# Layer 0's first convolution weights as seven products of quarters per chunk, with sums and bias on GpSimd and finer, interleaved stages

## The chip, the cores and the metric

The kernel runs on one core of a Trainium2 chip. The metric is the time of one execution in device microseconds (us). The five engines of the core are named as the profile names them: PE (matrix products; PEld is its weight load), DVE (VectorE), ACT (ScalarE), POOL (GpSimd) and SP (issues most DMAs). Each engine works through its own queue in order, and waits on semaphores for the others.

## The reference, cut to what matters

Four graph layers follow each other, each with a layer norm in front and a residual. Only layer 0 is touched, and of it only the first part: `x` has 128 graphs of 64 nodes with 256 features.

```python
h = jnp.maximum(_layernorm(x, axis=-1), 0.0)
# layer 0, _L0_gnn_ref(h, adj, Wg0, bg0, Wg1, bg1, ...)
h = relu(einsum('ts,bsh->bth', adj, x @ Wg0 + bg0))   # x is the normed h here
h = relu(einsum('ts,bsh->bth', adj, h @ Wg1 + bg1))
for p in range(1, 5):      # four small LSTMs over windows of p nodes
    ...
```

All numbers are float32. The 256x256 product with `Wg0` is what the change rewrites.

## The kernel before, in words

The 8192 rows (graph and node) are cut into 16 chunks of 512 (`NCH`, `CHUNK`). The first stage of the kernel, from its start to about 193 us, is the two graph convolutions of layer 0; then come layer 0's LSTMs, and layers 1, 2 and 3.

A chunk `n` goes through `graph_convolutions(n)`, a generator with five stages:

1. **norm**: `bn_stats`/`bn_aggr` (L87, L88) on DVE, a root on ACT (L95), two small DVE operations (L96, L97), and four scaled ReLUs on ACT (L109), which give `h`. Then the load of chunk `n + 3` is issued on SP.
2. **aggregate**: eight products of `h` with the block-diagonal adjacency `bdA` (128x128 each) into two PSUM banks, and two DVE copies of 128x512 to `aggT` (L145).
3. **first weights**: per half `c` of the output features two products of 128x512 with `wg0`; the bias comes in with DVE's `scalar_tensor_tensor` (L516, `rsum * bg0 + p`), then a ReLU on ACT (L524). The result is `h1T`.
4. **second weights**: eight products of 128x256 with `wg1`, two DVE additions of `bg1` (L539); the result `z` lies in `aggT`'s buffer.
5. **second aggregation**: eight products of `z` with `bdA`, two ReLUs on ACT (L555), and from chunk 8 on a DMA to `hmem`.

All these products stand in the profile as L50, the helper `mm`. The loop over `n` advances the newest chunk by one stage and then each older one by one stage, so that five chunks are under way. Between these steps it advances `tables`, generators that build lookup tables for layers 1 and 2, mostly with small and 128x512 operations on DVE, and some products on PE. At `n == 2` it issues the LSTM weights `Weights(...)`: three 1 MB loads, and for each four sums of 128x512 on POOL (L440). PSUM has eight banks, taken in turn by `bank()`. The order that is written down is not the order in which instructions stand: a scheduler reorders within each engine's queue, and after that each queue runs strictly in its order.

The LSTMs already use seven products of quarters (`gate`, L651), with sums of weights by the same four operations on POOL.

Of the kernel before, what the change touches and what calls it, by code (L numbers as in the profile page):

```python
# [9 lines left out]
F32 = mybir.dt.float32  # L10
# [3 lines left out]
ALU = mybir.AluOpType  # L14
AX = mybir.AxisListType

P = 128
T = 64
# [12 lines left out]
def gnn_stack_kernel(ctx: ExitStack, tc: tile.TileContext, a: dict, out: bass.AP):  # L31
    nc = tc.nc
    NTOK = out.shape[0]
    NCH = NTOK // CHUNK
# [8 lines left out]
    def bank():  # L43
        return psums["now"].tile([P, 512], F32, tag="bank", name="bank", bufs=psums["banks"])
# [4 lines left out]
    def mm(o, lhsT, rhs, start=True, stop=True):  # L49
        nc.tensor.matmul(o, lhsT, rhs, start=start, stop=stop)  # L50
# [75 lines left out]
    def quarter_sums(v, s):  # L126


        a11, a12, a21, a22 = v[:, 0, :, 0, :], v[:, 1, :, 0, :], v[:, 0, :, 1, :], v[:, 1, :, 1, :]
        for o, x, y, op in (  # L130
            (s[:, 0], a21, a22, ALU.add),
            (s[:, 1], s[:, 0], a11, ALU.subtract),
            (s[:, 2], a12, s[:, 1], ALU.subtract),
            (a21, a11, a21, ALU.subtract),
        ):
            nc.gpsimd.tensor_tensor(o, x, y, op)
        return {1: a11, 2: a12, 3: s[:, 2], 4: a22, 5: s[:, 0], 6: s[:, 1], 7: a21}

    def aggregate(h, bd, dst):

        for c in range(2):
            p = bank()
            for i in range(4):
                mm(p[:, i * P : (i + 1) * P], h[:, i, c * P : (c + 1) * P], bd)
            nc.vector.tensor_copy(dst[:, c, :], p)  # L145
# [269 lines left out]
    with ExitStack() as l0:  # L415
# [37 lines left out]
        with ExitStack() as conv:  # L453
            psums["now"] = conv.enter_context(
                tc.tile_pool(name="psum0", bufs=8, space=bass.MemoryType.PSUM, reuse_waits="tile")
            )

            def cpool(name, bufs):
                return conv.enter_context(tc.tile_pool(name=name, bufs=bufs, reuse_waits="tile"))

            xin = cpool("xin", 4)
            g0 = cpool("g0", 5)
            wc = cpool("wc", 1)
            hop = cpool("hop", 3)

            def load_x(n):
                xt = xin.tile([P, 4, D], F32, tag="xin", name="xin")
                nc.sync.dma_start(out=xt, in_=token_tiles(a["x"], n))
                return xt


            coming = {0: xin.tile([P, 4, D], F32, tag="xin", name="xin")}
            first_x = token_tiles(a["x"], 0)
            for i in range(4):
                nc.sync.dma_start(out=coming[0][:, i, :], in_=first_x[:, i, :])
            for src_, dst_ in (("adjT", adjT2), ("adj", adj2)):
                for h in range(2):
                    nc.scalar.dma_start(out=dst_[h * T : (h + 1) * T, :], in_=a[src_])
            coming[1] = load_x(1)
            wg0 = wc.tile([P, 2, D], F32, tag="wg0", name="wg0")  # L480
            nc.sync.dma_start(out=wg0, in_=a["Wg0"])
            bg0 = wc.tile([P, 2], F32, tag="bg0", name="bg0")
            nc.scalar.dma_start(out=bg0, in_=a["bg0"])
            wg1 = wc.tile([P, 2, D], F32, tag="wg1", name="wg1")
            nc.sync.dma_start(out=wg1, in_=a["Wg1"])
            bg1 = wc.tile([P, D], F32, tag="bg1", name="bg1")
            nc.scalar.dma_start(out=bg1, in_=a["bg1"].partition_broadcast(P))
            for n in (2, 3):
                coming[n] = load_x(n)
            nc.sync.dma_start(out=bias, in_=a["bih"])  # L490
            nc.sync.dma_start(out=bias2, in_=a["bhh"])
            for h in range(2):
                r = slice(h * T, (h + 1) * T)
                nc.gpsimd.tensor_copy(bdA[r, r], adjT2[r, :])

            rsum = wc.tile([P, T], F32, tag="rsum", name="rsum")
            p = bank()
            mm(p[:, :T], ones[:T, :], adjT2[:T, :])
            nc.vector.tensor_copy(rsum, p[:, :T])
            rsum_b = rsum.unsqueeze(1).to_broadcast([P, 8, T])  # L500

            def graph_convolutions(n):

                h = Norm(coming.pop(n), True).all()
                if 4 <= n + 3 < NCH:
                    coming[n + 3] = load_x(n + 3)
                yield
                aggT = g0.tile([P, 2, CHUNK], F32, tag="aggT", name="aggT")
                h1T = g0.tile([P, 2, CHUNK], F32, tag="h1T", name="h1T")
                aggregate(h, bdA, aggT)  # L510
                yield
                for c in range(2):
                    p = bank()
                    for k in range(2):
                        mm(p, wg0[:, k, c * P : (c + 1) * P], aggT[:, k, :], k == 0, k == 1)
                    nc.vector.scalar_tensor_tensor(  # L516
                        h1T[:, c, :].rearrange("p (b t) -> p b t", t=T),
                        rsum_b,
                        bg0[:, c : c + 1],
                        p.rearrange("p (b t) -> p b t", t=T),  # L520
                        ALU.mult,
                        ALU.add,
                    )
                    nc.scalar.activation(h1T[:, c, :], h1T[:, c, :], AF.Relu)  # L524
                yield
                z = aggT.rearrange("p c t -> p (c t)").rearrange("p (i d) -> p i d", i=4)
                for ip in range(2):
                    p = bank()
                    for i2 in range(2):
                        i = 2 * ip + i2  # L530
                        for k in range(2):
                            mm(
                                p[:, i2 * D : (i2 + 1) * D],
                                h1T[:, k, i * P : (i + 1) * P],
                                wg1[:, k, :],
                                k == 0,
                                k == 1,
                            )
                    nc.vector.tensor_tensor(  # L539
                        z[:, 2 * ip : 2 * ip + 2, :],  # L540
                        p.rearrange("p (i d) -> p i d", i=2),
                        bg1.unsqueeze(1).to_broadcast([P, 2, D]),
                        ALU.add,
                    )
                yield
                if n < NCH // 2:
                    col = n % 2 * CHUNK
                    dst = hTs0[n // 4][:, n % 4 // 2, :, col : col + CHUNK]
                else:
                    dst = hop.tile([P, 2, CHUNK], F32, tag="hop", name="hop")  # L550
                for c in range(2):
                    p = bank()
                    for i in range(4):
                        mm(p[:, i * P : (i + 1) * P], z[:, i, c * P : (c + 1) * P], bdA)
                    nc.scalar.activation(dst[:, c, :], p, AF.Relu)  # L555
                if n >= NCH // 2:
                    nc.sync.dma_start(out=hmem[n], in_=dst)

            tables = chain(edge_tables(), late_tables())
            under_way = []  # L560
            for n in range(NCH + 4):
                if n < NCH:
                    under_way.append(graph_convolutions(n))

                for one in under_way[-1:] + under_way[:-1] if n < NCH else list(under_way):
                    if next(one, 0) == 0:
                        under_way.remove(one)
                    if n >= 3:
                        next(tables, None)
                if n == 2:  # L570
                    weights["ih", 0], weights["ih", 1] = Weights("ih", 1), Weights("ih", 2)
                    weights["hh", 1] = Weights("hh", 2)
                    nc.vector.tensor_tensor(bias, bias, bias2, ALU.add)
            for _ in tables:
                pass
# [244 lines left out]
        for slot in range(len(tasks) + 2):  # L820
# [9 lines left out]
            if new:  # L830
                step = steps[new[0]]
                one = step.gate(new[1])
# [12 lines left out]
            if new:  # L845
                next(one)
                flight.append((new, one))
                at, k = new[0], new[2]
# [6 lines left out]
                if step.w == MAX_SKIP and step.t == 2 and k < 2 and step.g < NGR - 1:  # L855
                    for u in range(2):
                        n = 4 * step.g + 2 * u + k
                        later.append((slot, "x", n))
            while later and later[0][0] <= slot:
                _, kind, n = later.pop(0)  # L860
                residual[n] = fetch_x(n)
            next(norm_steps, None)
            while later_weights and later_weights[0][0] <= slot:
                _, ph = later_weights.pop(0)
# [23 lines left out]
    with ExitStack() as l1:  # L888
# [30 lines left out]
        for g, c in last_outs:  # L919
            for u in range(2):  # L920
                n = 4 * g + 2 * u + c
# [447 lines left out]
    with ExitStack() as l2:  # L1369
# [48 lines left out]
        with ExitStack() as dense2:  # L1418
# [60 lines left out]
            side, rights = {}, {}  # L1479
            NP = NCH // 2  # L1480
            with ExitStack() as first_dense:
# [40 lines left out]
                for slot, (pr, m2) in enumerate(tasks):  # L1522
                    n = slot + 3
                    one = first_layer(pr, m2)
# [92 lines left out]
            for pr in range(2, NP):  # L1617
# [4 lines left out]
                one = second_layer(pr, False)  # L1622
# [370 lines left out]
```

## Time and profile before

| what | value |
|---|---|
| time, median of 3 runs | 2060.63 us (2059.19 to 2062.6) |
| the profiled execution's own time | 2061.03 us |
| its span in the profile | 2059.3 us |
| granted TensorE clock, mean | 0.996 |
| busy share of the span: PE, DVE, ACT, POOL | 97%, 66%, 58%, 15% |
| last product of the convolutions starts | 190.82 us |
| first product of the LSTMs starts | 192.77 us |

The page gives busy times and shares, then the span in 40 slices, then groups of instructions. A group's row has the line, engine, operation and tiles, the number of instructions, the busy time and mean duration of one, and the idle time of the engine ahead of them with what ended it. A float32 product stands in the profile as two passes, so "x8" for products with `wg0` means four of them. The timeline gives start and duration; a row merges instructions of one kind. A product's duration holds its drain, so that the distance from one start to the next is the price of one.

### The profile page before, as it was taken

To read this page: it belongs to the slowest core of one execution; us is meant where nothing else is said; L and a number is where in the kernel's file an instruction comes from. 1 tells how busy PE (TensorE), PEld (TensorE's weight loads), DVE (VectorE), ACT (ScalarE), POOL (GpSimd) and SP (SyncE) were. 2 spreads that over 40 slices of the span, in tenths; PEclk is the share of its full clock that TensorE was granted. 3 is DMA by queue.
4 is the path that set the end of the run, shared out by engine and by line. 5 is a ranking of instruction groups with operands and counts; after the bars stand their busy time and mean duration, and the time that the engine had idled before them with its cause. 6 is when DMAs were issued, how large, how long until landed. Compare 5 with 4: busy or idle time off the path is not lost. (4 is left out here: it accounts for less than half of the span.)

```text
span 2059.3 us, 25491 instructions
## 1 busy us (share of the span) xinstructions
PE 2006.1 (97%) x9444; PEld 1346.1 (65%) x9444; DVE 1359.5 (66%) x2507; ACT 1184.4 (58%) x2230; POOL 308.2 (15%) x416
## 2 busy tenths in 40 slices
PE   8999999999999999999999999999999999999998
PEld 6777478866688845887667887333334775444786
DVE  8755666564565477566556555677777877886776
ACT  4344766555565457566446564666675556591544
POOL 3000010020110020002001000323223420000563
PEclk9999999999999999999999999999999999999999
DMA  9331000100100170001001003412223841022012
GB/s 316 98 98 51 0 21 1 42 0 1 41 1 1 40 246 21 1 0 42 0 1 41 1 16 120 138 61 97 72 98 122 298 154 52 0 82 82 32 62 72
DMA packets 63196, 135.06 MB, mean 66 GB/s; under 512 B 6240, under 2 KB 40928, under 8 KB 60768
## 3 DMA queue, kind: packets, MB, share of 16 engines
q1 hardware_dynamic: 56832, 109.11, 15.6%
q0 software_dynamic: 5632, 24.12, 3.1%
q8 instruction: 74, 1.21, 0.2%
q14 instruction: 50, 0.41, 0.1%
q10 hardware_dynamic: 608, 0.20, 0.0%
HBM read 87.28 MB, written 46.14 MB: 65 GB/s over the span
## 5 line engine op out<-in xcount | busy, mean ns | idle before, releaser
L651 PE MATMUL pa<-xop,sih 128*128 128x256 f32 (+2 forms) x1056 | 344.4, 418 | 11.7 <-DVE gate L705 8.2
L679 ACT ACTIVATE gate<-gate,bias 128x256 f32<-128x256 f32 (+2 forms) x368 | 247.4, 679 | 173.6 <-DVE gate L695 91.0
L651 PEld LDWEIGHTS pa<-xop,sih 128*128 128x128 f32 x1056 | 198.4, 190 | 87.9 <-issue 22.8
L651 PE MATMUL pc<-xop,wih 128*128 128x256 f32 (+2 forms) x736 | 251.2, 423 | 0.0
L695 DVE TENSOR_TENSOR gate<-pb,gate 128x256 f32<-128x256 f32 (+2 forms) x184 | 87.5, 475 | 225.7 <-PE pb L651 154.1
L651 PE MATMUL pa<-lstm_h,shh 128*128 128x256 f32 (+1 forms) x672 | 212.7, 398 | 0.0
L993 DVE SCALAR_TENSOR_TENSOR lr<-lr 128x1024 f32<-128x1024 f32 x128 | 151.1, 1222 | 55.3 <-ACT lr L992 55.3
L651 PEld LDWEIGHTS pc<-xop,wih 128*128 128x128 f32 x736 | 139.8, 190 | 51.2 <-issue 23.0
L710 DVE TENSOR_TENSOR gate<-pc,gate 128x256 f32<-128x256 f32 (+2 forms) x184 | 87.6, 476 | 121.2 <-PE pc L651 120.9
L992 ACT COPY lr<-pair 128x1024 f32<-128x1024 f32 x128 | 123.1, 1014 | 47.6 <-PE pair L986 47.6
L651 PEld LDWEIGHTS pa<-lstm_h,shh 128*128 128x128 f32 x672 | 127.7, 190 | 30.2
L651 PE MATMUL pc<-lstm_h,whh 128*128 128x256 f32 (+1 forms) x448 | 141.8, 398 | 0.0
L694 ACT COPY gate<-pa 128x256 f32<-128x256 f32 (+2 forms) x184 | 76.1, 413 | 96.7 <-PE pa L651 96.1
L986 PE MATMUL pair<-sd_hot,xq 64*128 64x512 f32 x512 | 127.5, 616 | 0.3 <-ACT lr L992 0.3
L705 DVE TENSOR_TENSOR gate<-pa,gate 128x256 f32<-128x256 f32 (+2 forms) x184 | 87.5, 475 | 44.0 <-PE pa L651 43.4
L970 PE MATMUL bank<-wlv,hT 128*128 128x512 f32 x240 | 110.7, 604 | 0.0
L699 ACT COPY gate<-pa 128x256 f32<-128x256 f32 (+2 forms) x184 | 75.4, 410 | 59.1 <-PE pa L651 57.9
L679 ACT ACTIVATE gate<-pa,bias 128x256 f32<-128x256 f32 (+2 forms) x184 | 94.0, 511 | 23.6 <-PE pa L651 22.0
L440 POOL TENSOR_TENSOR sih<-wih 128x512 f32<-128x512 f32 x8 | 10.7, 1335 | 630.6 <-DMA wih<-in_WihT 484.4
L651 PE MATMUL pa<-xop,wih 128*128 128x256 f32 (+1 forms) x320 | 101.4, 398 | 2.7 <-ACT xop L632 2.7
L651 PE MATMUL pb<-xop,wih 128*128 128x256 f32 (+1 forms) x320 | 100.3, 398 | 0.4 <-DVE gate L695 0.4
L651 PEld LDWEIGHTS pc<-lstm_h,whh 128*128 128x128 f32 x448 | 85.1, 190 | 20.1
(346 smaller groups left out, 3809.2 us busy)
## 6 DMA issues: line engine op xcount, KB each, us to landing
field<-sd_hot SPq DMA_DIRECT2D x4, 2304.0 KB, 17.2
wih<-in_WihT SPq DMA_DIRECT2D x8, 1024.0 KB, 5.1
xres<-in_x SPq DMA_DIRECT2D x16, 512.0 KB, 4.6
xa<-xres POOLq DMA_DIRECT2D x16, 512.0 KB, 5.2
dense<-field POOLq DMA_DIRECT2D x4, 2048.0 KB, 8.5
xin<-xb SPq DMA_DIRECT2D x16, 512.0 KB, 3.4
h<-xb SPq DMA_DIRECT2D x16, 512.0 KB, 3.2
xin<-in_x SPq DMA_DIRECT2D x15, 512.0 KB, 3.9
```

Source lines behind the costliest of these rows:

```text
L440: nc.gpsimd.tensor_tensor(o, x, y, op)
L651: ins = nc.tensor.matmul(p[:, : self.N], weights[kind, self.phase](k, q), x[k], start=first_ and kind == "ih", stop=kind == "hh" or not se ...
L679: nc.scalar.activation(out, in_, AF.Tanh if q == 2 else AF.Sigmoid, bias=bias[:, self.w - 1, 2 * q + j : 2 * q + j + 1],)
L694: nc.scalar.copy(blk[0, 0], pa[:, :N])
L695: nc.vector.tensor_tensor(blk[0, 0], pb[:, :N], blk[0, 0], ALU.add)
L699: nc.scalar.copy(blk[1, 0], pa[:, :N])
L705: nc.vector.tensor_tensor(blk[1, 1], pa[:, :N], blk[1, 1], ALU.add)
L710: nc.vector.tensor_tensor(blk[1, 0], pc[:, :N], blk[1, 0], ALU.add)
L970: ins = nc.tensor.matmul(p, hTs[n][:, k, i * P : (i + 1) * P], wlv[:, k, :], start=k == 0, stop=k == 1)
L986: ins = nc.tensor.matmul(p[:, par, :], queries[it][r, c * P : (c + 1) * P], sd_hot[r, :], start=True, stop=True)
L992: nc.scalar.copy(lr, p)
L993: nc.vector.scalar_tensor_tensor(lr, lr, 0.2, lr, ALU.mult, ALU.max)
```

## The change

The product with `wg0` is done by Strassen's scheme in Winograd's form. `wg0` is cut into four 128x128 quarters, and `aggT` into four blocks of 128x256 (feature half by half of the chunk's columns). Seven products of 128x128 by 128x256 take the place of eight that the four products of 128x512 amount to.

- `quarter_sums` makes the sums of the weights once, four POOL operations of 128x128.
- Per chunk POOL makes four differences of 128x256 into `side`.
- Per chunk three ACT copies, four DVE additions and three POOL additions of 128x256 take the place of the two `scalar_tensor_tensor`. The bias `rb = rsum * bg0` is made once on DVE in two operations on 128x64, ahead of all else that DVE does for the chunks, and is added to three blocks on POOL and to the fourth by DVE.
- Three of the seven products use the bank `pa` one after the other without a restart (`start=False`), after it has been copied or read.
- The generator has twelve stages: the norm is four, the first weights are four, the second aggregation two. `order` says which chunk is advanced when: 2 means chunk `n - 2`. In a round the products run as 1 and 2; half of the last stage of `n - 4`; 6 and 7; its other half; the aggregation of `n - 1`; 5; the second weights of `n - 3`; 4 and 3.

```diff
+            rb = wc.tile([P, 2, T], F32, tag="rb", name="rb")
+            for c in range(2):
+                nc.vector.tensor_scalar(rb[:, c, :], rsum, bg0[:, c : c + 1], None, ALU.mult)
+            s_g0 = wc.tile([P, 3, 1, P], F32, tag="s_g0", name="s_g0")
+            left = quarter_sums(wg0.rearrange("p k (q j m) -> p k q j m", q=1, j=2), s_g0)
...
-                h = Norm(coming.pop(n), True).all()
+                norm = Norm(coming.pop(n), True)
...
                 aggregate(h, bdA, aggT)
-                yield
-                for c in range(2):
-                    p = bank()
-                    for k in range(2):
-                        mm(p, wg0[:, k, c * P : (c + 1) * P], aggT[:, k, :], k == 0, k == 1)
-                    nc.vector.scalar_tensor_tensor(
...
+                for o, x, y in (
+                    (0, b12, b11),
+                    (2, b22, side[:, 0]),
+                    (1, b22, b12),
+                    (3, b21, side[:, 2]),
+                ):
+                    nc.gpsimd.tensor_tensor(side[:, o], x, y, ALU.subtract)
+                right = {1: b11, 2: b21, 3: b22, 4: side[:, 3], 5: side[:, 0], 6: side[:, 2], 7: side[:, 1]}
+                yield
...
+                product(1, pa, True)
+                product(2, pb, True)
+                nc.scalar.copy(blk[0, 0], pa)
+                nc.vector.tensor_tensor(blk[0, 0], pb, blk[0, 0], ALU.add)
+                biased(0, blk[0, 0])
+                yield
+                product(6, pa)
+                nc.scalar.copy(blk[1, 0], pa)
+                biased(1, blk[1, 0])
+                product(7, pc, True)
+                nc.scalar.copy(blk[1, 1], pc)
+                biased(1, blk[1, 1])
+                yield
+                product(5, pa)
+                nc.vector.tensor_tensor(blk[1, 1], pa, blk[1, 1], ALU.add)
+                yield
+                product(4, pc)
+                nc.vector.tensor_tensor(blk[1, 0], pc, blk[1, 0], ALU.add)
+                product(3, pa)
+                nc.vector.tensor_tensor(
+                    nodes4(blk[0, 1]), nodes4(pa), rb[:, 0].unsqueeze(1).to_broadcast([P, 4, T]), ALU.add
+                )
+                for c in range(1, -1, -1):
                     nc.scalar.activation(h1T[:, c, :], h1T[:, c, :], AF.Relu)
...
+            order = (2, 0, 4, 0, 2, 4, 1, 0, 2, 3, 0, 2)
             for n in range(NCH + 4):
...
+                for at, back in enumerate((0, 0, 0, 0) + tuple(b for b in order if b) if n < 4 else order):
+                    if n - back in chunks:
+                        next(chunks[n - back])
+                    if n >= 3 and back and at % 2 == 0:
                         next(tables, None)
```

`biased(c, blk)` is POOL's `tensor_tensor` of a block with `rb[:, c]`, repeated over four graphs. The pool `g0s` holds two `side` tiles.

More of the change, by code (lines that the diff above doesn't have):

```diff
@@ L462, in gnn_stack_kernel @@
             g0 = cpool("g0", 5)
+            g0s = cpool("g0s", 2)
             wc = cpool("wc", 1)
@@ L499, in gnn_stack_kernel, with nodes4 @@
             nc.vector.tensor_copy(rsum, p[:, :T])
-            rsum_b = rsum.unsqueeze(1).to_broadcast([P, 8, T])
-            def graph_convolutions(n):
-                h = Norm(coming.pop(n), True).all()
+            rb = wc.tile([P, 2, T], F32, tag="rb", name="rb")
[3 more added lines that the diff above has]
+            left = quarter_sums(wg0.rearrange("p k (q j m) -> p k q j m", q=1, j=2), s_g0)
+            def nodes4(ap):
+                return ap.rearrange("p (b t) -> p b t", t=T)
+            def graph_convolutions(n):
+                norm = Norm(coming.pop(n), True)
+                for step in range(2):
+                    for i in range(2):
+                        norm.stats(2 * step + i)
+                    if step:
+                        norm.roots()
+                    yield
+                for step in range(2):
+                    for i in range(2):
+                        norm.scaled(2 * step + i)
+                    yield
                 if 4 <= n + 3 < NCH:
                     coming[n + 3] = load_x(n + 3)
-                yield
+                h = norm.h
                 aggT = g0.tile([P, 2, CHUNK], F32, tag="aggT", name="aggT")
@@ L510, in graph_convolutions @@
                 aggregate(h, bdA, aggT)
-                yield
-                for c in range(2):
-                    p = bank()
-                    for k in range(2):
-                        mm(p, wg0[:, k, c * P : (c + 1) * P], aggT[:, k, :], k == 0, k == 1)
[L516 to L522, printed above, removed]
-                    )
+                side = g0s.tile([P, 4, 256], F32, tag="side", name="side")
@@ new lines, in graph_convolutions @@
+                b11, b21, b12, b22 = (
+                    aggT[:, k, u * 256 : (u + 1) * 256] for u in range(2) for k in range(2)
+                )
[7 more added lines that the diff above has]
+                right = {1: b11, 2: b21, 3: b22, 4: side[:, 3], 5: side[:, 0], 6: side[:, 2], 7: side[:, 1]}
@@ new lines, in graph_convolutions, with product, biased @@
+                yield
+                def product(k, p, first_=False):
+                    nc.tensor.matmul(
+                        p, left[k][:, 0, :], right[k], start=first_, stop=True, skip_group_check=True
+                    )
+                def biased(c, blk):
+                    nc.gpsimd.tensor_tensor(
+                        nodes4(blk), nodes4(blk), rb[:, c].unsqueeze(1).to_broadcast([P, 4, T]), ALU.add
+                    )
+                pa, pb, pc = (bank()[:, :256] for _ in range(3))
@@ new lines, in graph_convolutions @@
+                blk = {(c, u): h1T[:, c, u * 256 : (u + 1) * 256] for c in range(2) for u in range(2)}
+                product(1, pa, True)
[8 more added lines that the diff above has]
+                product(7, pc, True)
@@ new lines, in graph_convolutions @@
+                nc.scalar.copy(blk[1, 1], pc)
[3 more added lines that the diff above has]
+                nc.vector.tensor_tensor(blk[1, 1], pa, blk[1, 1], ALU.add)
+                yield
+                product(4, pc)
[3 more added lines that the diff above has]
+                    nodes4(blk[0, 1]), nodes4(pa), rb[:, 0].unsqueeze(1).to_broadcast([P, 4, T]), ALU.add
+                )
@@ L555, in graph_convolutions @@
                     nc.scalar.activation(dst[:, c, :], p, AF.Relu)
+                    if c:
+                        break
+                    yield
                 if n >= NCH // 2:
                     nc.sync.dma_start(out=hmem[n], in_=dst)
+                yield
             tables = chain(edge_tables(), late_tables())
-            under_way = []
+            chunks = {}
+            order = (2, 0, 4, 0, 2, 4, 1, 0, 2, 3, 0, 2)
             for n in range(NCH + 4):
                 if n < NCH:
[L563 to L568, printed above, removed]
+                    chunks[n] = graph_convolutions(n)
+                for at, back in enumerate((0, 0, 0, 0) + tuple(b for b in order if b) if n < 4 else order):
+                    if n - back in chunks:
+                        next(chunks[n - back])
+                    if n >= 3 and back and at % 2 == 0:
                         next(tables, None)
```

## The prediction

> **What bounds the kernel now.** The page comes first: PE is busy all the time, POOL hardly.
>
> ```profile
> PE 2006.1 (97%) x9444; PEld 1346.1 (65%) x9444; DVE 1359.5 (66%) x2507; ACT 1184.4 (58%) x2230; POOL 308.2 (15%) x416
> ```
>
> The change lies wholly in the convolutions, so PE's timeline there is next. One round of a middle chunk:
>
> ```profile
> 147.32 3.62 PE L50 MATMUL bank<-wg,h1T 128*128 128x256 f32 x16
> 150.77 3.60 PE L50 MATMUL bank<-aggT,wg 128*128 128x512 f32 x8
> 154.21 1.95 PE L50 MATMUL bank<-bdA,h 128*128 128x128 f32 x16
> 155.99 1.95 PE L50 MATMUL bank<-bdA,aggT 128*128 128x128 f32 x16
> 157.78 3.62 PE L50 MATMUL bank<-wg,h1T 128*128 128x256 f32 x16
> ```
>
> The reader is to see that rows follow without idle time: 3.45 + 3.44 + 1.78 + 1.79 = 10.46 us a chunk, all of it PE. From 52 to 192 us PE is busy 140.00 of 140 us by the windows view. So each microsecond taken from PE there is gained, if nothing else becomes late. The groups give the prices of what moves:
>
> ```profile
> L50 PE MATMUL bank<-aggT,wg 128*128 128x512 f32 x128 | 58.5, 598 | 1.4 <-DVE aggT L145 1.4
> L516 DVE SCALAR_TENSOR_TENSOR h1T<-rsum,bg,bank 128x512 f32<-128x512 f32 x32 | 23.8, 743 | 19.4 <-PE bank L50 19.3
> L136 POOL TENSOR_TENSOR w1S<-w1T,w1S 128x256 f32<-128x256 f32 x1 | 1.7, 1704 | 0.0
> L136 POOL TENSOR_TENSOR w1S<-w1T 128x256 f32<-128x256 f32 x1 | 0.7, 723 | 2.5 <-DMA w1T<-in_W1T 2.5
> ```
>
> Last come two views of the kernel's start: the timeline (start, duration), and the DMA issues (the last number is the time to landing).
>
> ```profile
> 4.02 0.42 DVE L87 BATCH_NORM_STATS2 ln_st<-xin 128x6 f32<-128x256 f32 x1
> 7.49 0.34 SPq L491 DMA_DIRECT2D bias<-in_bhh  x1
> 17.64 1.28 POOL L440 TENSOR_TENSOR sih<-wih 128x512 f32<-128x512 f32 x1 [12.85 <-DMA wih<-in_WihT]
> 30.67 1.64 DVE L309 SCALAR_TENSOR_TENSOR wide<-wide,iota 128x512 f32<-128x512 f32 x1
> 31.73 1.71 POOL L440 TENSOR_TENSOR shh<-whh,shh 128x512 f32<-128x512 f32 x1
> ```
>
> ```profile
> bg<-in_bg ACTq DMA_DIRECT2D x1, 1.0 KB, 4.2
> ```
>
> `bg0` is issued at 3.26 us and lands 4.2 later, at 7.5. POOL sums the LSTM weights from 17.64 to 33.4 us, twelve operations of 1.27 us back to back; today nobody waits for them there.
>
> **Products.** Eight passes of 128x512 at 0.43 become fourteen of 128x256 at 0.2145 (the x16 row: 3.45/16): 3.43 becomes 3.00, so 0.43 a chunk, 6.9 us in all. That is 0.33%; about 0.2% (4.1 us) is what a measurement of this kernel can tell from no change.
>
> **DVE, ACT, POOL per chunk.** DVE: two L516 (1.49) become four 128x256 additions out of PSUM (0.42 each by the LSTMs' L695): 1.68. ACT: three copies of 0.37 more (L694), to about 6 us. POOL: seven operations of 0.72 (L136 undisturbed): 5.0 us. Each fits into 10 us; the queues' order is what matters.
>
> **The start.** In the changed program's order the two `rb` operations stand on DVE ahead of the first `bn_stats`, and they wait for `bg0`: stats start at 7.7 instead of 4.02, and the first product at 11.5 instead of 7.75. Part of that is covered, since today the second `aggT` copy (end 14.62) waits behind the sum of the LSTM biases, which waits for its DMA until 13.83. PE's first aggregation, 3.9 us as today, ends at 15.5; the second copy ends at 16.4. So 1.8 of the 3.7 reach POOL.
>
> From there POOL's queue holds, in order: differences of chunk 0, two weight sums, three biases of chunk 0, two sums, differences of chunk 1, then eight sums between the biases of chunk 1 and the differences of chunk 2. Added up from 16.4: chunk 0's differences end at 18.6, its biases at 23.3, chunk 1's differences at 28.7, its last bias at 38.0, chunk 2's difference for product 7 at 43.3. PE must follow: product 3 of chunk 0 waits for the addition behind the last bias (23.8; PE was free at 21.9); product 6 of chunk 1 until 27.3; product 3 of chunk 1 until 38.4 (free at 34.5), with the second weights of chunk 0 between. Behind that bias DVE stands as well, and when it goes on, L306, L309 and L311 come between the additions that give `z` of chunk 0; at today's 1.36, 1.64 and 1.23 its second half is there at 44.5. Then 0.45 (rest of an aggregation), 0.86, 0.89, 1.79, 0.43, 3.43, 0.86: product 3 of chunk 2 ends at 53.3. By then four aggregations, three first weights, two second weights and one last stage are done. Today this state is reached at 38.27. Arrears: 15.0 us. Bounds: 50 (no contention, `z` not late: 51.5, and a quicker start) to 57 (POOL sums at 1.7 where DVE collides, and the clock, below).
>
> **The rounds after.** 13 chunks remain: 13 x 0.43 = 5.6 us back. Today's stall at 42.13 (1.47, a ReLU late) falls into the arrears: 1.5 more. New is a chain inside a round. Product 6 accumulates in the bank of product 1 and waits for ACT's copy of it. In most rounds both ReLUs of the chunk before stand ahead of that copy on ACT, and their additions behind the second `z` addition on DVE. From the end of the second weights: 0.21 to the result, 0.61 to the next DVE start, 0.42 addition, 0.03, 0.56 and 0.56 for the two ReLUs (0.63 less overlap), 0.37 copy, 0.06: 2.82 us. PE has meanwhile products 4, 3, 1, 2 and half of a last stage: 1.72 + 0.89 = 2.61. So 0.2 late, in about ten rounds: 2 us. In five or six rounds table operations stand between the two `z` additions and push this by 0.35 to 0.65: 2.5 more. I take 5 us for 13 rounds; bounds 0 and 12.
>
> **Contention of POOL and DVE.** L309 takes 1.64 beside POOL where L364, alike in form, takes 0.74 alone: +0.90 against a POOL operation of 1.27, so about 0.5 against one of 0.72. L516 (0.73 at 17.63), copies and stats ran beside the same sums at their usual durations, and POOL's at 1.27. So only the 27 table operations that read SBUF by two inputs or fast (L328, L331, L361, L364 and others) pay; with POOL busy half the time 27 x 0.5 x 0.5 = 6.6 us of DVE, of which a third stands ahead of a `z` addition; that is in the 5.
>
> The Trainium skill (SBUF — State Buffer, section "SBUF: two separate sides") says that DVE and GpSimd lock a shared port pair, and the loser blocks for the whole of the other's instruction. By that rule the 27 would pay up to 27 x 0.72 = 19 us of DVE time, and the rounds some 6 instead of 2 us.
>
> **The clock.** PE will idle for 2 to 4 us several times before 45 us. After an idle time of 3.1 us this trace has, in the timeline and in the windows view (PE, PEld, DVE, ACT, POOL busy, then the granted clock):
>
> ```profile
> 724.89 1.25 PE L167 MATMUL bank<-ident,hT 128*128 128x128 f32 x8 [3.10 <-DVE xres L172]
> ```
>
> ```profile
> 724.00:730.00 6.00, 5.11 (x15) 2.83 (x16) 3.79 (x7) 0.59 (x1) 1.06 (x2) 0.72 0.96 314
> ```
>
> The granted clock falls to 0.72 over the window, and work worth 3.1 us takes 4.9. While POOL is the last to arrive this costs nothing; at the end of the arrears it is up to 1.8, which is in the upper bound.
>
> The Trainium skill (TensorE: Matmul & The Clock Gate, Part 1) gives about 3.4 us of idling as the point of return to half clock. By it most of these waits are too short and would cost nothing; the row has 3.1 paying.
>
> **The sum.** 15.0 - 5.6 - 1.5 + 5 = +12.9 us where the LSTMs begin (192.77 today); they are as full of PE work as before, so nothing is given back. Tail: the last chunks' chains have 1.79 of other products in them, 0.2 at most. The profiled execution took 2061.03 (span 2059.3); 2061.0 + 12.9 = 2073.9, and 0.4 less against the median of 2060.63: 2073.5 us.
>
> **Rivals.** *Faster: the arrears are hidden.* If POOL's queue did not hold PE, only the late `bg0` would stay: 1.8 to 3.7 - 5.6 - 1.5 and no slip = -3.4 to -5.3 us, about 2056. It decides from the state of 38.27 being reached before 45.4. For it: PE's rounds have room, and POOL is at 15%. Against: twelve sums and eighteen small operations are 28 us of POOL in a queue that starts at 16.4. *POOL or DVE becomes the bound.* If POOL's small operations run at the 1.70 of the collided L136, seven are 11.9 us, over a round of 10.2; in the ten rounds with tables that is 1.7 each, 17 us on top of 7.9 (the sum without its 5 us of slips): 2085. Against: the undisturbed sums beside stats and PSUM copies. *The saving and the arrears cancel.* Arrears of 9, slip 0: +2, 2062. It needs the sums' landing and order to be kinder than the queue shows.
>
> **Numbers.** Forecast 0.70; POOL or DVE bound 0.15; cancelling 0.07; faster 0.08. From these slower by over 0.2% is 0.86, within 0.2% 0.06, faster 0.08. The range: arrears 50 - 38.3 = 11.7, slip 0: 11.7 - 7.1 = +4.6; arrears 18.7, slip 12: +23.6. So 2064 to 2084; it leaves out the faster and cancelling cases and the far end of the bound one.
>
> **What would show it.** Right: first `bn_stats` after 7.5; POOL without a gap from 16 to 43 us; PE idle before a product 3 near 38 and in the 40s, released by DVE or POOL; the LSTMs' first product near 205.7; middle rounds of 10.2 to 10.5 instead of 10.46, with the idle time ahead of product 6 released by ACT. Wrong: that state reached before 45, rounds near 10.0, or POOL rows of 1 us and more in the middle rounds.

## The result, and the profile after

The changed kernel takes 2076.25 us (median of 6 runs, 2074.48 to 2077.65); the kernel before took 2061.51 beside it. The ratio is 1.0071, interval 1.0058 to 1.0084: slower by 14.7 us, where 2073.5 in a range of 2064 to 2084 was forecast. The profiled execution took 2077.65 us, span 2075.7.

PE's busy time, in the page of the kernel after, has hardly moved:

```profile
PE 2009.6 (97%) x9540; PEld 1371.6 (66%) x9540; DVE 1367.0 (66%) x2541; ACT 1198.3 (58%) x2278; POOL 388.2 (19%) x532
```

The reader should not read from this that nothing was saved: a PE that runs at half clock for a while is busy longer (from 43.65 us on, below). POOL's 80 us more are in the main the 112 small operations, 83 us by their groups. Two of the three groups show that they ran near the price expected, 0.72 us (the number behind the comma is the mean in ns):

```profile
L551 POOL TENSOR_TENSOR h1T<-h1T,rb 128x256 f32<-128x256 f32 x48 | 35.6, 759 | 57.8 <-DVE h1T L560 52.6 <-ACT h1T L564 5.0
L541 POOL TENSOR_TENSOR side<-aggT,side 128x256 f32<-128x256 f32 x32 | 23.8, 744 | 3.7 <-DVE aggT L145 3.0 <-DVE ln_rs L96 0.2
```

The start is where the time goes. The timeline of DVE after (start, duration) has the bias products ahead of the first statistics, waiting for a DMA:

```profile
7.61 0.42 DVE L504 TENSOR_SCALAR rb<-rsum,bg 128x64 f32<-128x64 f32 x2 [3.49 <-DMA bg<-in_bg]
7.94 0.42 DVE L87 BATCH_NORM_STATS2 ln_st<-xin 128x6 f32<-128x256 f32 x1
```

The timeline of POOL after, in part: the weight sums (L440) stand between a chunk's differences (L541) and its biases (L551), and no row here has idle time ahead of it.

```profile
30.66 1.27 POOL L440 TENSOR_TENSOR sih<-sih,wih 128x512 f32<-128x512 f32 x1
31.89 1.27 POOL L440 TENSOR_TENSOR wih<-wih 128x512 f32<-128x512 f32 x1
33.11 1.27 POOL L440 TENSOR_TENSOR sih<-wih,sih 128x512 f32<-128x512 f32 x1
34.34 0.73 POOL L541 TENSOR_TENSOR side<-aggT 128x256 f32<-128x256 f32 x1
35.02 0.73 POOL L551 TENSOR_TENSOR h1T<-h1T,rb 128x256 f32<-128x256 f32 x1
35.71 1.27 POOL L440 TENSOR_TENSOR shh<-whh 128x512 f32<-128x512 f32 x1
36.94 0.72 POOL L551 TENSOR_TENSOR h1T<-h1T,rb 128x256 f32<-128x256 f32 x1
```

PE's timeline after, from the first of these waits to the state that before reached at 38.27 (product 3 of chunk 2 done, here 55.47):

```profile
24.00 0.70 PE L546 MATMUL bank<-aggT,s_g 128*128 128x256 f32 x2 [1.55 <-DVE h1T L571]
27.48 1.22 PE L546 MATMUL bank<-side,s_g 128*128 128x256 f32 x2 [2.78 <-POOL side L541]
...
38.17 0.70 PE L546 MATMUL bank<-aggT,s_g 128*128 128x256 f32 x2 [0.98 <-DVE h1T L571]
38.71 1.03 PE L546 MATMUL bank<-aggT,wg 128*128 128x256 f32 x4
41.49 0.71 PE L50 MATMUL bank<-bdA,aggT 128*128 128x128 f32 x4 [1.76 <-DVE aggT L595]
43.65 1.22 PE L50 MATMUL bank<-bdA,aggT 128*128 128x128 f32 x4 [1.45 <-DVE aggT L595]
44.67 1.06 PE L546 MATMUL bank<-side,wg 128*128 128x256 f32 x2
45.52 1.19 PE L546 MATMUL bank<-side,s_g 128*128 128x256 f32 x2
46.50 1.92 PE L50 MATMUL bank<-bdA,aggT 128*128 128x128 f32 x8
48.21 2.68 PE L50 MATMUL bank<-bdA,h 128*128 128x128 f32 x16
50.72 0.60 PE L546 MATMUL bank<-side,s_g 128*128 128x256 f32 x2
...
55.04 0.59 PE L546 MATMUL bank<-aggT,s_g 128*128 128x256 f32 x2
```

The brackets show the queue: products wait for DVE's addition behind a bias (L571), for a difference (L541), for `z` (L595). And from 43.65 on the same products take about twice as long: two passes of 128x256 1.06 where they take 0.59 later. The windows view after says why (PE, PEld, DVE, ACT, POOL busy, then the granted clock):

```profile
43.00:45.00 2.00, 1.35 (x5) 1.35 (x6) 1.97 (x5) 0.98 (x2) 1.27 (x2) 0.50 0.97 295
45.00:47.00 2.00, 2.00 (x7) 1.34 (x7) 1.91 (x6) 1.45 (x5) 1.03 (x2) 0.50 1.07 372
47.00:49.00 2.00, 2.00 (x11) 2.00 (x11) 1.88 (x9) 0.67 (x2) 1.25 (x2) 0.50 1.09 387
```

A middle round after, from PE's and ACT's timelines; 160.46 to 170.83 is one round, 10.37 us instead of 10.46:

```profile
160.46 1.05 PE L50 MATMUL bank<-bdA,aggT 128*128 128x128 f32 x8
161.60 0.67 PE L546 MATMUL bank<-side,s_g 128*128 128x256 f32 x2
...
170.83 1.05 PE L50 MATMUL bank<-bdA,aggT 128*128 128x128 f32 x8
```

```profile
170.42 1.15 ACT L580 ACTIVATE h1T<-h1T 128x512 f32<-128x512 f32 x2 [2.97 <-DVE h1T L574]
171.47 0.35 ACT L559 COPY h1T<-bank 128x256 f32<-128x256 f32 x1
```

Half of a last stage is worth 0.89 us, and product 6 comes 1.14 after its start: 0.25 of waiting, for a copy that stands behind two ReLUs. The LSTMs begin at 206.47 instead of 192.77: 13.7 us later. Another 1.2 us are lost in pieces until 2034 us, and some 1.5 at the very end, where the kernel's last product runs at another clock in the two traces. PE's timeline before, then after:

```profile
2052.29 2.00 PE L50 MATMUL pair<-wh,field 128*128 128x256 f32 x8 [0.90 <-ACT field L1860]
```

```profile
2067.06 3.63 PE L50 MATMUL pair<-wh,field 128*128 128x256 f32 x8 [0.91 <-ACT field L1922]
```

The granted clock there was 1.00 before and 0.50 after, behind the same waits (0.57 and 0.90, 0.58 and 0.91). It is not the change that makes this: the kernel before with its sums moved, a control below, has 3.62 us there too, and six of the other kernels, the first four below among them, have 2.00.

### The profile page after: what moved, and what is told of

The parts are those of the page before. It is cut to its first block, busy times and chain, and to the rows that moved or that the text cites. A ratio compares the mean times of both kernels' runs of the same rounds, so it can differ in the third digit from the quotient of the medians.

```text
span 2075.7 us, 25969 instructions
## 1 busy us (share of the span) xinstructions
PE 2009.6 (97%) x9540; PEld 1371.6 (66%) x9540; DVE 1367.0 (66%) x2541; ACT 1198.3 (58%) x2278; POOL 388.2 (19%) x532
## 3 DMA queue, kind: packets, MB, share of 16 engines
q8 instruction: 75, 1.23, 0.2%
## 5 line engine op out<-in xcount | busy, mean ns | idle before, releaser
L440 POOL TENSOR_TENSOR sih<-wih 128x512 f32<-128x512 f32 x8 | 10.3, 1292 | 564.5 <-PE pa L713 353.0
```

## The experiments

Beside the first four of these kernels the kernel before took 2061.9 us, beside the later ones, on other chips, 2069.8 and 2070.6. So ratios to the kernel before are compared; 0.001 is 2.1 us. "First product" is the first aggregation, "LSTMs" their first product. "State" is the moment at which the second aggregation of chunk 1 starts. With seven products in the new order, products 1 and 2 of chunk 3 stand ahead of it, so 0.87 us come off before a row is compared with the 38.27 of before (after: 55.47); with the old products in the new order half of a first-weights stage does, 1.72 us. In "bias products later" 0.66 of waiting comes on top, and in "seven products, old order" product 3 of chunk 2 is still to come.

| kernel | first product | state | LSTMs | ratio, interval |
|---|---|---|---|---|
| before | 7.75 | 38.27 | 192.77 | 1 |
| after | 12.18 | 56.34 | 206.47 | 1.0071 (1.0058 to 1.0084) |
| sums in round 8 | 12.04 | 43.88 | 198.28 | 1.0027 (1.0017 to 1.0036) |
| bias products later | 7.77 | 49.60 | 202.93 | 1.0035 (1.0021 to 1.0049) |
| both | 7.75 | 42.68 | 197.20 | 1.0024 (1.0014 to 1.0033) |
| new order, old products | 7.81 | 46.58 | 197.60 | 1.0012 (1.0002 to 1.0022) |
| seven products, old order | 12.35 | 54.97 | 222.54 | 1.0145 (1.0130 to 1.0161) |
| before, sums in round 8 | 7.74 | 38.39 | 192.26 | 1.0002 (0.9992 to 1.0011) |
| one sum a round | 7.86 | 40.32 | 193.11 | 1.0002 (0.9993 to 1.0011) |
| the same, old order | 7.84 | 44.75 | 213.28 | 1.0104 (1.0089 to 1.0119) |
| one sum a round, early bias | 12.19 | 44.45 | 196.94 | 1.0011 (1.0002 to 1.0020) |
| copy before the ReLUs | 7.78 | 40.55 | 190.14 | 0.9982 (0.9973 to 0.9992) |

My theory: the loss is made in the first 55 us, by the weight sums in POOL's queue and by the wait for `bg0`; the products themselves give their 0.43 us a round, less the wait for product 1's copy. Rivals: the order of stages costs by itself; POOL or DVE are too slow in every round.

**The sums out of the start.**

```diff
                 if n == 2:
-                    weights["ih", 0], weights["ih", 1] = Weights("ih", 1), Weights("ih", 2)
-                    weights["hh", 1] = Weights("hh", 2)
                     nc.vector.tensor_tensor(bias, bias, bias2, ALU.add)
+                if n == 8:
+                    weights["ih", 0], weights["ih", 1] = Weights("ih", 1), Weights("ih", 2)
+                    weights["hh", 1] = Weights("hh", 2)
```

> The changed kernel, with the loads and sums of the LSTM weights issued in round 8 instead of round 2; the sum of the LSTM biases stays in round 2. Theory (GpSimd's in-order queue makes the arrears at the start: twelve weight sums of 1.27 us stand between the small operations): GpSimd is free between 16 and 43 us, product 3 of chunk 2 ends near 44 us instead of 55.5, and the time falls by about 11 us, to 2065 (2062 to 2068). Rival A (the finer, interleaved order of stages costs the start, whatever GpSimd does): 2074 to 2077. Rival B (the small differences and biases on GpSimd are themselves too slow a link): GpSimd's waits stay, 2072 to 2077.

2067.28 us: 9 us of the 14.7 are gone, and the state is reached 12.5 us earlier. The queue holds most of the loss. (The loads of these weights move with their sums, but between 4 and 56 us no product of the changed kernel waits for a DMA itself, and DVE waits for one only at `bg0`.)

**The bias products later.** The two `rb` operations go behind chunk 0's scaled ReLUs, kept in program order.

```diff
-            for c in range(2):
-                nc.vector.tensor_scalar(rb[:, c, :], rsum, bg0[:, c : c + 1], None, ALU.mult)
...
+                if n == 0:
+                    for c in range(2):
+                        late(nc.vector.tensor_scalar(rb[:, c, :], rsum, bg0[:, c : c + 1], None, ALU.mult))
```

> The changed kernel, with the two rb operations issued after the norm of chunk 0 instead of ahead of it. Theory: the first statistics start at 4.0 us again and the first product near 8.4, but GpSimd's first difference only some 1 to 2 us earlier, and behind GpSimd nothing else moves: 2074.5 (2073 to 2076). Rival (the late bg0 is the larger part of the loss): 4 us or more less, 2072 or below.

2069.47 us: 7.4 us less, where I expected 2 of them. The first product moved by 4.4 us, the state by 6.7. The timeline of POOL in this kernel shows that more than the wait has changed, since the scheduler put chunk 2's differences (L542 here) ahead of the last four sums instead of behind them:

```profile
33.05 1.40 POOL L552 TENSOR_TENSOR h1T<-h1T,rb 128x256 f32<-128x256 f32 x2
34.41 1.41 POOL L542 TENSOR_TENSOR side<-aggT 128x256 f32<-128x256 f32 x2
35.77 1.59 POOL L542 TENSOR_TENSOR side<-aggT,side 128x256 f32<-128x256 f32 x2
37.33 1.71 POOL L440 TENSOR_TENSOR shh<-whh 128x512 f32<-128x512 f32 x1
```

So this run does not give the price of the wait alone: the number is the rival's, but its cause is not shown, and the 7.4 us need not be the wait's.

**Both.**

> The changed kernel, with both: weight sums in round 8, rb behind the norm of chunk 0. Theory: with nothing of the arrears but the chain of small steps left, the saving of the products shows: 2061 (2058 to 2064). Rival A (order of stages): 2070 or more.

2066.52 us, hardly better than the sums alone, and 5 us above the expectation. The timeline of POOL in this kernel shows the sums that were written in round 8: the scheduler pulled them forward, and they stand in a row again, now ahead of chunk 4's biases (L552):

```profile
68.00 1.28 POOL L440 TENSOR_TENSOR sih<-sih,wih 128x512 f32<-128x512 f32 x1
69.25 1.71 POOL L440 TENSOR_TENSOR wih<-wih 128x512 f32<-128x512 f32 x1
70.92 1.45 POOL L440 TENSOR_TENSOR sih<-wih,sih 128x512 f32<-128x512 f32 x1
72.33 0.91 POOL L552 TENSOR_TENSOR h1T<-h1T,rb 128x256 f32<-128x256 f32 x1
...
78.93 1.86 POOL L552 TENSOR_TENSOR h1T<-h1T,rb 128x256 f32<-128x256 f32 x2
```

```profile
81.30 0.70 PE L547 MATMUL bank<-aggT,s_g 128*128 128x256 f32 x2 [1.01 <-DVE h1T L572]
```

PE's row is the product that waits for the addition behind those biases. The two rounds there took 16.74 and 12.38 us instead of 13.92 and 11.07: 4.1 us, the same stall moved to another place.

**The order alone.** The twelve stages and `order` of the change with the old products and `scalar_tensor_tensor`; no POOL work per chunk.

```diff
-                h = Norm(coming.pop(n), True).all()
+                norm = Norm(coming.pop(n), True)
...
-            under_way = []
+            order = (2, 0, 4, 0, 2, 4, 1, 0, 2, 3, 0, 2)
```

> The new order of stages alone: products with Wg0, bias by DVE and the weight sums in round 2 as before the change, but twelve stages in the new order. Theory: without small GpSimd operations nobody waits for GpSimd, and the order by itself costs at most a few us: 2062 (2060 to 2066). Rival A (the order makes the loss): 2070 to 2077.

2065.74 us, ratio 1.0012: at the far end of what was expected. The order costs about 2.5 us (0.4 to 4.5) where the products do not need it; in its trace (2066.34 us) the LSTMs begin 4.8 us later. The loss is made at the start: the same work as before at 38.27 is done at 44.86 (46.58 less 1.72), and from there to the LSTMs it takes 152.7 us, before 154.5.

**One sum a round.** To settle what kept "both" at 2066.5. `put_off` collects the twelve sums; the bias products stand late as above, and the LSTM's bias sum in round 14.

```diff
+                if n == 4:
+                    sums = []
+                    weights["ih", 0], weights["ih", 1] = Weights("ih", 1, sums), Weights("ih", 2, sums)
+                    weights["hh", 1] = Weights("hh", 2, sums)
+                if n == 14:
+                    late(nc.vector.tensor_tensor(bias, bias, bias2, ALU.add))
+                if n >= 5 and sums:
+                    late(nc.gpsimd.tensor_tensor(*sums.pop(0)))
```

> The changed kernel with the bias products behind chunk 0's normalisation, the sum of the LSTM's biases in round 14, and the twelve weight sums kept in program order, one in each of rounds 5 to 16, in place of twelve in a row. Theory A (the kernel with both edits lost its second gain to the block of twelve sums, which the program's order put at 60.8 to 79.0 us ahead of chunk 4's bias additions: its rounds there took 16.74 and 12.38 us where the changed kernel's took 13.92 and 11.07, which is 4.1 us): 2066.5 less 4.1 is 2062.4 us, and up to 1.5 less where the sum of the LSTM's biases no longer holds up the second aggregation copy: 2061 to 2063, no round with over 1 us of waiting behind chunk 3, and the LSTM's first product at 191.5 to 193.5. Theory B (the table operations on VectorE between the two additions of a chunk make that wait, with or without weight sums): 2066 us, as the kernel with both edits.

1.0002: as fast as before, and LSTMs at 193.11. The block of sums was the rest. One detail missed: two waits of 1.2 us are left in later rounds, at 101.71 us for `z` (L599) and at 126.36 for the copy of product 1.

**A control.** The same move of the sums in the kernel before.

> The kernel before, with the loads and sums of the LSTM's weights written in round 8 instead of round 2 (its only work on GpSimd in this stage). A control for the kernels that move these sums: theory says that nobody waits for GpSimd in the kernel before, so the time stays at 2061.9 us (2060 to 2064). If it falls by more than 1 us, the sums already cost the kernel before something, by the table operations on VectorE that run beside them, and what the moved sums gained in the changed kernel is not all the queue on GpSimd.

1.0002: no difference. The sums cost nothing where nobody else needs POOL.

**The stages undone,** once in the changed kernel and once with the edits of one sum a round:

```diff
-                norm = Norm(coming.pop(n), True)
...
+                h = Norm(coming.pop(n), True).all()
...
-            order = (2, 0, 4, 0, 2, 4, 1, 0, 2, 3, 0, 2)
+            under_way = []
```

> The changed kernel with the chunk's stages undone: seven products, differences and biases as changed, but each chunk in the old five stages with the old loop over the chunks; the weight sums stay in round 2 and the bias products where the change put them. Theory A (the new order of stages costs the 2.5 us that the order-only kernel lost against before, and gives nothing back): about 2074 us, 2 us under the changed kernel (2071 to 2076), and the LSTM's first product 2 to 4 us earlier than 206.47. Theory B (the finer stages are what keeps the seven products from waiting for their own copies, differences and additions): at least 0.5 us more of waiting in each of 16 rounds, so 2080 us or more. Under A the difference between this kernel and before is the price of the products with their queue on GpSimd.

> The same edits as in the kernel with one sum a round, in the old five stages and the old loop over the chunks: seven products with nothing else left of the change. Theory A (the seven products save 0.43 us in each of 16 rounds once GpSimd's queue and the early bias products are out of their way, and the new order's 2.5 us lie in the filling of the pipeline alone): 2061.9 less 5 to 7 is 2055 to 2057 us, faster than the kernel before. Theory B (without finer stages the products wait for their own copies and additions within the round): 0.3 to 0.7 us in each of 16 rounds, so 2060 to 2068 us. The pair with the kernel of one sum a round gives the price of the order.

1.0145 and 1.0104. Theory A fell in both. The first is 15 us over after, as theory B has it (2080 or more); the second is 21 over the kernel with one sum a round (19 by the medians), more than theory B allowed. A round in the second of them, from PE's timeline, takes 11.25 to 12 us near the end:

```profile
171.70 0.70 PE L540 MATMUL bank<-aggT,s_g 128*128 128x256 f32 x2 [0.89 <-DVE h1T L563]
172.23 1.05 PE L50 MATMUL bank<-bdA,h 128*128 128x128 f32 x8
173.12 1.95 PE L50 MATMUL bank<-bdA,aggT 128*128 128x128 f32 x16
174.91 3.62 PE L50 MATMUL bank<-wg,h1T 128*128 128x256 f32 x16
...
183.39 0.70 PE L540 MATMUL bank<-aggT,s_g 128*128 128x256 f32 x2 [0.89 <-DVE h1T L563]
```

Product 3, the last of the seven, waits 0.89 us in these rounds for DVE's addition of product 5 (L563), which has to come after a copy on ACT and a bias on POOL. From 60 to 192 us these waits come to 5.8 us, those for the copy of product 1 to 4.4 and those for POOL's differences to 1.3, where the kernel with one sum a round waits 3.3 in all. All seven stand together in one stage, with too little other work between. So the finer stages, which cost the old products 2.5 us, are worth 15 to 21 to the new ones (the stages and the order were undone together, so their shares are not known).

**The wait for `bg0` alone.** One sum a round, with the bias products where the change put them.

> The changed kernel with its bias products where the change put them, ahead of the first statistics, but the twelve weight sums one a round in rounds 5 to 16 and the LSTM's bias sum in round 14: against the kernel with one sum a round, only the wait for the layer's bias is put back. Theory A (the first chunk's delay is mostly taken up while the pipeline fills, as the pair with and without it and the sums in a block showed: second aggregation of chunk 1 at 43.88 and 42.68 us for first products at 12.04 and 7.75): 1 to 2 us over the kernel with one sum a round, ratio 1.0007 to 1.0012. Theory B (with the queue on GpSimd gone the whole 4.3 us by which the first product starts later reaches the end): ratio about 1.0023.

1.0011 against 1.0002, 1.9 us as theory A has it; but in the two traces the LSTMs begin 3.8 us apart, nearer to theory B. The intervals of the ratios overlap. The wait costs 2 to 4 us; which, these runs do not settle.

**The copy before the ReLUs.** On top of one sum a round.

```diff
+                yield
                 for c in range(1, -1, -1):
-                    nc.scalar.activation(h1T[:, c, :], h1T[:, c, :], AF.Relu)
+                    late(nc.scalar.activation(h1T[:, c, :], h1T[:, c, :], AF.Relu))
                 yield
...
                         next(chunks[n - back])
+                    if at == (4 if n < 4 else 0) and n - 3 in chunks:
+                        next(chunks[n - 3])
```

> The kernel with one sum a round, and chunk n-1's two ReLUs moved behind the copy of chunk n's product 1 on ScalarE (a stage of their own, kept in program order). In that kernel the steady rounds take 10.37 us where the cleanest takes 10.05, and the trace shows the copy at 158.11 us behind two ReLUs (157.05 for 1.15 us), though its product had ended by about 157.2; TensorE idles 3.6 us between 60 and 192 us. Theory A (these ReLUs are what product 6 waits for in the steady rounds): 10.04 us in the last six rounds and 1.5 to 3 us less in all, so the ratio to the kernel before falls from 1.0002 to 0.9988 to 0.9995, at or just beyond what the measurement can tell from none. Theory B (another step in the round ends as late, such as the four biases and differences on GpSimd or the second ReLU in front of the next product): the rounds stay at 10.37 us, ratio 1.0002.

0.9982, 3.7 us faster than before, the only kernel of the study whose interval lies below 1. From 1.0002 that is 4.1 us where theory A had 1.5 to 3; in the traces the LSTMs begin 3.0 earlier, and the two intervals are wide enough for either. The timelines of ACT and PE in it:

```profile
165.28 0.37 ACT L563 COPY h1T<-bank 128x256 f32<-128x256 f32 x1 [4.09 <-PE bank L550]
165.55 1.15 ACT L585 ACTIVATE h1T<-h1T 128x512 f32<-128x512 f32 x2
```

```profile
165.51 1.05 PE L50 MATMUL bank<-bdA,aggT 128*128 128x128 f32 x8
166.40 0.60 PE L550 MATMUL bank<-side,s_g 128*128 128x256 f32 x2
...
175.56 1.05 PE L50 MATMUL bank<-bdA,aggT 128*128 128x128 f32 x8
```

Product 6 now follows after exactly the 0.89 of the half stage, and the round is 10.05 us: the 0.43 saved of 10.46, less 0.02.

## Why the prediction was right, point by point

- **Products.** The round from 56.34 to 66.38 takes 10.04 us, those with the copy first 10.05, against 10.03: right. (3.45/16 is 0.2156 and not 0.2145, which makes the saving 0.41 a chunk and the round 10.05.)
- **The wait for `bg0`.** First stats 7.94 (7.7 forecast), first product 12.18 (11.5). That 1.8 of the 3.7 reach the path is not confirmed: 2 to 4 us with the queue cleared.
- **POOL's queue.** Right step by step: the first product 3 held up at 24.00 (23.8), product 6 of chunk 1 at 27.48 (27.3), its product 3 at 38.17 (38.4), chunk 2's difference for product 7 done at 43.58 (43.3), the second half of `z` at 43.6 (44.5). Only the way to that `z` was another: L306 and L309 stand ahead of both its additions, and between them stand L311, L315 and L339; L306 and L311 took 1.13 and 0.63 us instead of 1.36 and 1.23. One sum a round removes the queue: from 1.0071 to 1.0011 with the bias products still early, 12.4 us (the LSTM's bias sum moved as well).
- **The arrears, 15.0 forecast, 17.2 measured (55.47 less 38.27): the failed step is the clock.** I put it at nothing in the sum and at up to 1.8 in the upper bound. From 43.65 to 50.72 PE spent 7.07 us on work that takes 3.99 at full clock (0.45, 0.43, 0.43, 0.89, 1.79 from its later rows): 3.1 us, less 0.9 by which `z` came sooner. An earlier half-clock stretch, from 25.8 to 32.7 us by the windows, did cost nothing, as argued, since POOL's bias was later still: PE waited another 0.98 us for it at 38.17.
- **The rounds after.** 17.2 fell to 13.7: 3.5 given back. Of 5.6 + 1.5 that is 3.6 of slips, where I had 5. Their cause is shown for the copy behind the ReLUs: product 6 waits 0.25 for it here, and moving it took the ratio from 1.0002 to 0.9982. What is left in that kernel between 60 and 192 us is 2.2 us of idle PE, all in waits for `z` (L600, 2.2 in three). That table operations on DVE lie ahead of those additions was not tested by itself.
- **The rivals.** "POOL or DVE bound" fell with means of 744 and 759 ns per POOL operation, far from 1.70. "Faster, if the queue did not hold PE" named the right condition, but not the whole price: with the queue gone and `bg0` out of the way the kernel is level with before, since the same work is done 1.2 us later (40.32 less 0.87, against 38.27) and only 0.8 of the 7.1 is made up from there. That is 6.3 us of slips, more than the 3.6 of the changed kernel; the two waits of 1.2 us are part of it, and what the twelve spread sums cost there was not tested. "Saving and arrears cancel" fell with arrears of 17.2 instead of 9. I gave the order itself no price; with the old products it has one of about 2.5 us.
- **The sum.** +13.7 us at the LSTMs against +12.9. It holds two errors of opposite sign, 2.2 too little for the arrears and 1.4 too much for the slips, so that it comes so close is in part luck. Behind the LSTMs' start I added nothing; the traces have 1.2 there and the last product's clock.

The Trainium skill (TensorE: Matmul & The Clock Gate, Part 1) was weighed with its about 3.4 us of idling before half clock. This case speaks against using it as a threshold for one wait: the clock fell to 0.50 during the second of two waits of 1.55 and 2.78 us, and again of 1.76 and 1.45, each pair with less than 1 us of work between.

The Trainium skill (SBUF — State Buffer, "SBUF: two separate sides") would by the prediction's estimate have put some 6 us of port lock into the rounds. The changed kernel does not show that much: all its slips together are 3.6 us.

## What to carry to other kernels

An engine with 15% of busy time can still be the bound of a stage: add up its queue in its real order from the moment it starts, and look for work that is urgent to nobody (here twelve weight sums) between operations that the critical engine waits for. Spread such work and keep it in program order, since a scheduler may pull a block forward again. Splitting one product into several short dependent ones paid here only where each dependent step had other PE work between it and its source, down to which copy stands first on ACT.

## What the runs showed of the hardware that I had not expected

The granted clock fell without any idle time of 3 us. Two waits of 1.5 to 2.8 us close together were enough; in the kernel with the new order and old products one of 2.27 us was, at 34.77 us, and in "bias products later" two of 0.66 and 1.20, behind which the clock fell at 52.35. Yet a wait of 1.89 us in "the same, old order" (up to 22.56 us) cost no clock.

The moments of the change tell more than the lengths of the waits. By windows of 0.25 us the clock of the changed kernel fell at 25.83 and 42.90 us and rose at 32.66 and 49.73; that of "bias products later" fell at 35.28 and 52.35 and rose at 38.70 and 55.77. Within a trace these moments lie whole multiples of 3.41 us apart (2, 3 and 2; 1, 4 and 1). Taken as steps of 3.41 us, the step ahead of each of these falls holds 1.9 to 3.1 us of idle PE, in one wait or several, and the step ahead of each rise holds none. The wait of 1.89 us lies across an edge of its trace's steps, with 1.5 us at most in one. So what seems to count is the idle time within a step whose edges the program does not choose; that would also fit the last product, which runs at either clock behind the same waits. This is read from the traces; no run shifted a wait to test it.

After each of the falls in the changed kernel the clock stayed at 0.50 for 6.8 us, the last 5.2 and 6.1 of them without a gap in PE's work. A stall is thus paid for a second time after it ends: here 3.1 us behind waits of 3.2.
